# One product of two neighbouring row pairs, split once more into seven of its own quarters, in a graph network's matrix products

## The chip, the cores and the metric

The kernel runs on one core of one Trainium2 chip. The metric is the device time of one execution in microseconds (us), lower being better. TensorE multiplies matrices, VectorE (DVE in the profile), ScalarE (ACT) and GpSimd (POOL) do the rest; SyncE (SP), ACT and POOL issue DMA transfers.

## The reference

One layer of a relational graph network over 1250 nodes with 1024 features, 20000 edges of 8 types, followed by a gate; all f32.

```
h   = max(layernorm(x), 0)
u   = h @ root + bias
for r in 8 types:
    u += mean over edges of type r into each node (h[src]) @ weight[r]
z   = concat(u, h) @ w_gate + b_gate
out = x + tanh(u) * z + h * (1 - z)
```

## The kernel before, in words

The kernel multiplies first and gathers afterwards: `h` is multiplied by ten matrices of 1024 x 1024 (the eight `weight[r]`, `root`, and the half of `w_gate` that meets `h`), the products of the eight types are stored as rows in HBM (`y`, three groups of types), and rows are then gathered per edge, weighted and added into `u`. An eleventh matrix (the other half of `w_gate`) multiplies `u` at the end and is not in the loop that is changed.

**Tiling.** The 1250 nodes are 10 blocks of 128 (the last of 98). A step (s, i) multiplies matrix s (0 to 9) with pair i (0 to 4) of blocks i and i + 5, so 256 rows. Every step uses Winograd's form of Strassen's scheme: the 256 x 1024 left side and the 1024 x 1024 right side are cut into quarters, and `product` (L195) makes seven products of a 128 x 512 by a 512 x 512 quarter or sum of quarters, where a plain one takes eight. `h_op[i]` holds the left sides, transposed, under the names A11, A12, A22, S1 to S4 (A12 is block i with the second half of the features); `Factors` (L121) holds the right sides in seven buffers of 1 MB (`place`: b11, b21, b22, t1 to t4), and has two buffers more, `spare`. A matrix's b11 and t3 (which first holds b12) are loaded into the spare buffers of the matrix before (`load_first`, L134), its b22 and b21 into buffers of the matrix before as those come free. `make_t1` to `make_t4` are subtractions of whole quarters on VectorE.

**A product's order.** `product` works through A11, S1, S2, S4, S3, A12, A22. Each is four f32 matmuls of 512 columns, each of which the hardware runs as two instructions. Sums that share partial results stay in a bank of PSUM and are read in between:

```
add(b, A11, True);  copy c11 <- b      (ACT)
add(c, S1, True);   copy c22 <- c      (ACT)
add(b, S2);         copy c12 <- b      (ACT)
add(c, S4);         c12 += c           (DVE)
add(b, S3);         copy d <- b (ACT);  c22 += d (DVE)
add(a, A12, True);  c11 += a           (DVE)
add(b, A22);        copy c21 <- b      (ACT)
```

`bank()` hands out six PSUM banks in turn. The results c11 to c22 lie in two row tiles of 512 KB (`rows`, four buffers, two per step), which SP's queue stores when the step is over.

**Order of the work beside it.** Engines run their queues in the order in which the program issues instructions; that order is written by hand. After each of the seven products, `product` calls `between(j)`, in which `step` (L257) issues the handling of the next matrix and then a share of other work. In the first 440 us that is the indexing of the edges (counts and ranks, on ACT, VectorE, GpSimd and some small matmuls); after it the gathering, in which `spread` (L910) deals slots of edges over the calls: GpSimd issues an indirect DMA that gathers rows into one of four `got` buffers, and VectorE multiplies them with a weight and adds (L866). The number of calls left is counted as 7 per step. `step` calls `load_first` for the next matrix in the first step of a matrix (i = 0, j = 3); `load_b22`, `make_t1`, `load_b21` with `make_t2`, and `make_t3` come in the last step (i = 4, j = 0, 1, 3 and 4), `make_t4` at j = 0 of the next matrix's first step. All loads but those of the first matrix go through ACT's queue.

Of the kernel before, what the change touches and what calls it, by code (L numbers as in the profile page):

```python
# [9 lines left out]
F32 = mybir.dt.float32  # L10
# [9 lines left out]
def tile_rgcn_highway(  # L20
# [38 lines left out]
    KC = D // P  # L59
    KQ = KC // 2  # L60
    Q = D // 2
    ND = -(-N // P)
    NP = ND // 2
    NCH = -(-E // P)
    EL = E - (NCH - 1) * P
    G = 3
    R0 = (0, 3, 6, R)
    K = ((20, 10, 8, 7, 7, 6, 5, 5, 4, 3), (20, 10, 8, 7, 7, 6, 5, 5, 4, 3),
         (16, 7, 6, 5, 4, 4, 3, 3, 2, 2))
# [10 lines left out]
    A11, A12, A22, S1, S2, S3, S4 = range(7)  # L80
# [4 lines left out]
    def nrows(d):  # L85
        return min(P, N - d * P)
# [10 lines left out]
    rows = ctx.enter_context(tc.tile_pool(name="rows", bufs=4))  # L97
# [5 lines left out]
    hr_dram = dram.tile([N, D], F32, name="hr_dram")  # L103
    z_dram = dram.tile([N, D], F32, name="z_dram")
# [4 lines left out]
    y = [dram.tile([(R0[g + 1] - R0[g]) * N, D], F32, name=f"y{g}") for g in range(G)]  # L109
# [5 lines left out]
    def bank():  # L115
        return psum.tile([P, 512], F32, name="ps", bufs=6)
# [4 lines left out]
    class Factors:  # L121
# [3 lines left out]
        def __init__(self, w, old=None):  # L125
            self.w, self.old = w, old

        def load(self, i, j, to):
            queue = nc.scalar if self.old else nc.sync
            queue.dma_start(to, self.w[i * Q:(i + 1) * Q, j * Q:(j + 1) * Q]  # L130
                            .rearrange("(k p) n -> p k n", p=P))
            return to

        def load_first(self):  # L134
            old = self.old
            if old is None:
# [12 lines left out]
            self.load(0, 0, p["b11"])  # L149
            self.load(0, 1, p["t3"])  # L150

        def load_b22(self):
            self.load(1, 1, self.place["b22"])
# [16 lines left out]
        def make_t4(self):  # L170
            p = self.place
            nc.vector.tensor_sub(p["t4"], p["b21"], p["t2"])

    def transposed(aop, part, of, n):

        for half, to in enumerate(((A11, A12), (A21, A22))[part]):
            p = bank().rearrange("p (k f) -> p k f", k=KQ)
            for i in range(KQ):
                k = KQ * half + i
                nc.tensor.transpose(p[:, i, :n], of[:n, k * P:(k + 1) * P], ident[:n, :n])  # L180
            copy = nc.vector.tensor_copy if half else nc.scalar.copy
            copy(aop[:, to, :, :n], p[:, :, :n])  # L182
            if n < P:
                nc.gpsimd.memset(aop[:, to, :, n:], 0.0)

    def left(aop, part=0):

        if part != 3:
            nc.vector.tensor_add(aop[:, S1], aop[:, A21], aop[:, A22])
            nc.vector.tensor_sub(aop[:, S2], aop[:, S1], aop[:, A11])  # L190
        if part != 1:
            nc.vector.tensor_sub(aop[:, S4], aop[:, A12], aop[:, S2])
            nc.vector.tensor_sub(aop[:, S3], aop[:, A11], aop[:, A21])

    def product(aop, w, to, between=lambda j: None, last=None, pieces=1):  # L195

        c11, c12 = to[0][:, :Q], to[0][:, Q:]
        c21, c22 = to[1][:, :Q], to[1][:, Q:]  # L200
        step = [0]

        def add(b, i, fresh=False, at=slice(0, Q)):
            for k in range(KQ):
                nc.tensor.matmul(b[:, at], aop[:, i, k, :], w.of[i][:, k, at],  # L205
                                 start=(fresh and k == 0), stop=(k == KQ - 1),
                                 skip_group_check=True)

        def done():
            between(step[0])  # L210
            step[0] += 1

        b, c = bank(), bank()
        add(b, A11, True)
        nc.scalar.copy(c11, b)  # L215
        done()
        add(c, S1, True)
        nc.scalar.copy(c22, c)  # L218
        done()
        add(b, S2)  # L220
        nc.scalar.copy(c12, b)  # L221
        done()
        add(c, S4)
        nc.vector.tensor_add(c12, c12, c)  # L224
        done()
        add(b, S3)
        d = rows.tile([P, Q], F32, name="part", bufs=2)
        nc.scalar.copy(d, b)  # L228
        nc.vector.tensor_add(c22, c22, d)  # L229
        done()  # L230
        a = bank()
        add(a, A12, True)
        nc.vector.tensor_add(c11, c11, a)  # L233
        done()
        if pieces == 1:
            add(b, A22)
            if last:
                last(b, 0)
            else:
                nc.scalar.copy(c21, b)  # L240
        else:
            last(d, 0)
            for j in range(pieces):
                at = slice(j * Q // pieces, (j + 1) * Q // pieces)
                b = bank()
                add(b, A22, True, at)
                last(b[:, at], at.start, d[:, at])
        done()

    mats = [weight[r] for r in range(R)] + [root, w_gate[D:, :], w_gate[:D, :]]  # L250
    ROOT = R
    NM = len(mats)
    fac = []
    for w in mats:
        fac.append(Factors(w, fac[-1] if fac else None))

    def step(s, i, between=lambda j: None):  # L257

        def beside(j):
            new = fac[s + 1]  # L260
            if i == 0 and j == 0 and s > 0:
                fac[s].make_t4()
            if i == 0 and j == 3:
                new.load_first()
            if i == NP - 1:
                if j == 0:
                    new.load_b22()
                elif j == 1:
                    new.make_t1()
                elif j == 3:  # L270
                    new.load_b21()
                    new.make_t2()
                elif j == 4:
                    new.make_t3()
            between(j)

        t = [rows.tile([P, D], F32, name="row") for _ in range(2)]
        product(h_op[i], fac[s], t, between=beside)
        for part in range(2):
            d = i + part * NP  # L280
            n = nrows(d)
            at = slice(d * P, d * P + n)
            if s >= ROOT:
                to = (hr_dram, z_dram)[s - ROOT][at, :]
                nc.vector.tensor_add(t[part], t[part], bias_bc)
            else:
                g = max(k for k in range(G) if R0[k] <= s)
                o = (s - R0[g]) * N + d * P
                to = y[g][o:o + n, :]
            nc.sync.dma_start(to, t[part][:n])  # L290

    steps = iter([(s, i) for s in range(NM - 1) for i in range(NP)])

# [17 lines left out]
    h_op = [keep.tile([P, 7, KQ, P], F32, name=f"h_op{i}") for i in range(NP)]  # L311
# [58 lines left out]
    with ExitStack() as early:  # L370
# [20 lines left out]
        class Normed:  # L391
# [80 lines left out]
        for name, of, pad in (("dst", dst, G * KEYS), ("typ", etype, R), ("src", src, 0)):  # L472
            t = ix0.tile([P, 2, P], I32, name=f"e_{name}")
# [359 lines left out]
    with ExitStack() as edges_part:  # L833
        gpool = edges_part.enter_context(tc.tile_pool(name="gpool", bufs=GOT))
        upool = edges_part.enter_context(tc.tile_pool(name="upool", bufs=4))
        bias_bc = edges_part.enter_context(tc.tile_pool(name="bpool", bufs=1)).tile(
            [P, D], F32, name="bias_bc")
# [113 lines left out]
        def beside(e, total, s, i, last):  # L951


            between = spread(e, total, 7 * ((last - s) * NP + NP - i))
            while s <= last:
                step(s, i, between)
                s, i = next(steps, (NM, 0))
            return s, i
# [109 lines left out]
        def in_turn(*es):  # L1068
            for e in es:
                yield from e  # L1070
# [62 lines left out]
        def held():  # L1133

            new, old = [], []
            for _ in edges(LG, range(HELD), lambda d, u: new.append(add_hr(d, u))):
                yield
                for add in old:
                    add()
                old, new[:] = new[:], []  # L1140
            for add in old + new:
                add()

        late = edges(LG, range(HELD, ND), to_last)
        between = spread(in_turn(late, held()), sum(K[LG]) + 2, 7 * ((NM - 2 - s) * NP + NP - i))
        while s < NM - 1:
            def beside_h(j):
                between(j)
# [69 lines left out]
```

## Time and profile before

| | |
|---|---|
| median of 3 runs | 1381.52 us (1381.38 to 1381.53) |
| profiled execution, own time | 1381.64 us |
| its span, first to last instruction | 1379.8 us |
| TensorE matmuls busy (PE) | 1363.0 us, 99% |
| TensorE weight loads (PEld) | 616.9 us, 45% |
| VectorE (DVE) | 861.7 us, 62% |
| ScalarE (ACT) | 339.6 us, 25% |
| GpSimd (POOL) | 627.2 us, 45% |
| DMA | 272.73 MB, mean 198 GB/s |
| granted TensorE clock | 0.999 |

How to read the profile's rows: a group's row gives the line of the code, the engine, the operation, what is written <- what is read, the shape, the count; then the busy time in us and the mean ns of one; then the engine's idle time just before these instructions and who ended it. In a timeline row the first two numbers are the start and the duration in us, and the bracket holds the idle time before it with its releaser. Matmul records overlap[...].

### The profile page before, as it was taken

The numbers are of one execution on the slowest core, as the hardware profiler recorded it, in microseconds if no ns is written. First come the engines' busy times: TensorE is split into PE (matmuls) and PEld (weight loads), VectorE is DVE, ScalarE is ACT, GpSimd is POOL, SyncE is SP. The second block draws the span as 40 slices with busy tenths as digits, with TensorE's granted clock in tenths as the row PEclk, the third lists the DMA queues.
The fourth block names the chain that finished last, engine by engine and source line by source line (L and its number), as shares of the span: only waits on it lengthen the run. The fifth ranks groups of instructions, "written<-read, shape, count | busy, mean of one in ns | idle before, by whom it ended". The sixth has DMA issues, their size and how long they took to land.

```text
span 1379.8 us, 11992 instructions
## 1 busy us (share of the span) xinstructions
PE 1363.0 (99%) x3570; PEld 616.9 (45%) x3570; DVE 861.7 (62%) x1662; ACT 339.6 (25%) x721; POOL 627.2 (45%) x567
## 2 busy tenths in 40 slices
PE   7999999999999999999999999999999999999997
PEld 3444444444444444444444444444444444444443
DVE  6956867886768625455355485544447564557985
ACT  3335655565521111111111111111111111121220
POOL 0003655665552624556575364544426433425641
PEclk9999999999999999999999999999999999999999
DMA  8754765684645256368868656777759845656861
GB/s 302 285 203 98 172 147 114 155 181 120 101 112 173 67 166 203 77 212 198 247 225 319 203 206 246 262 286 278 251 165 333 299 158 176 206 176 234 293 201 57
DMA packets 110007, 272.73 MB, mean 198 GB/s; under 512 B 25906, under 2 KB 27936, under 8 KB 109808
## 3 DMA queue, kind: packets, MB, share of 16 engines
q0 software_dynamic: 48864, 128.60, 29.0%
q1 hardware_dynamic: 39952, 101.38, 24.9%
q10 hardware_dynamic: 21120, 41.95, 9.7%
q8 instruction: 28, 0.46, 0.2%
q14 instruction: 43, 0.35, 0.1%
HBM read 214.20 MB, written 80.65 MB: 214 GB/s over the span
## 4 chain that ended last, share of the span: by engine, by line
PE 79%; issue 7%; DVE 4%; DMA 2%; POOL 2%; ACT 1%; POOLq 0%; DVEq 0%; ACTq 0%
PE ps L205 78%; POOL got L315 1%; DMA got<-y,idx 1%; DMA w<-in_L_gnn_weight_dram 1%; DMA got<-hr_dram,node 1%; PE ps_n L605 1%; DVE row L1166 0%; DVE h_op L1103 0%; POOL out_dram L321 0%; DVE u L1066 0%; DVE row L1167 0%; PE ps_q L656 0%; DVE h_op L182 0%; DVE u L866 0%; DVE w L1103 0%
## 5 line engine op out<-in xcount | busy, mean ns | idle before, releaser
L205 PE MATMUL ps<-w,h_op 128*128 128x512 f32 (+1 forms) x3088 | 1342.4, 593 | 0.0
L205 PEld LDWEIGHTS ps<-w,h_op 128*128 128x128 f32 x3088 | 580.2, 190 | 692.7 <-issue 688.7
L866 DVE SCALAR_TENSOR_TENSOR u<-got,w_of,u 128x1024 f32<-128x1024 f32 (+1 forms) x192 | 245.9, 1282 | 213.2 <-DMA got<-y,idx 209.3
L858 POOL DMA_INDIRECT got<-y,idx x202 | 248.2, 1228 | 236.1 <-DVE u L866 149.9
L684 POOL DMA_INDIRECT table<-row_col,at_i x157 | 175.9, 1121 | 149.0 <-DVE at_i L680 69.7
L224 DVE TENSOR_TENSOR row<-row,ps 128x512 f32<-128x512 f32 x55 | 37.5, 683 | 105.8 <-PE ps L205 61.0
L228 ACT COPY part<-ps 128x512 f32<-128x512 f32 x55 | 32.2, 585 | 269.7 <-PE ps L205 266.7
L240 ACT COPY row<-ps 128x512 f32<-128x512 f32 x50 | 29.3, 585 | 251.9 <-PE ps L205 233.7
L215 ACT COPY row<-ps 128x512 f32<-128x512 f32 x55 | 32.1, 584 | 168.3 <-PE ps L205 146.0
L221 ACT COPY row<-ps 128x512 f32<-128x512 f32 x55 | 32.1, 584 | 137.8 <-PE ps L205 132.2
L218 ACT COPY row<-ps 128x512 f32<-128x512 f32 x55 | 32.1, 584 | 131.8 <-PE ps L205 125.9
L229 DVE TENSOR_TENSOR row<-row,part 128x512 f32<-128x512 f32 x55 | 37.9, 688 | 41.9 <-ACT part L228 39.7
L670 DVE SCALAR_TENSOR_TENSOR junk<-k_bc,key_col,before 128x128 f32<-128x128 int32 x157 | 54.9, 350 | 4.2
L321 POOL DMA_INDIRECT u_dram<-u,node x20 | 30.0, 1499 | 59.9 <-DVE u L866 55.3
L352 POOL DMA_INDIRECT node_dram<-ids,pos_i x30 | 37.3, 1244 | 38.6 <-issue 38.3
L610 DVE TENSOR_TENSOR seen<-seen,ps_n 128x110 f32<-128x110 f32 x157 | 42.1, 268 | 15.5 <-PE ps_n L605 10.9
L587 ACT ACTIVATE is_lo<-io,less_lo 128x128 bf16<-128x128 f32 x157 | 50.1, 391 | 0.8 <-DVE row L229 0.8
L738 DVE SCALAR_TENSOR_TENSOR junk<-v_bc,val,one 128x1280 bf16<-128x1280 f32 x30 | 46.5, 1551 | 3.9 <-DMA v_bc<-val_dram 3.2
L233 DVE TENSOR_TENSOR row<-row,ps 128x512 f32<-128x512 f32 x55 | 37.5, 682 | 18.3 <-PE ps L205 16.5
L315 POOL DMA_INDIRECT u<-u_dram,node x20 | 22.3, 1113 | 56.7 <-DMA u_dram<-u,node 41.9
L160 DVE TENSOR_TENSOR w<-w,w 128x2048 f32<-128x2048 f32 x11 | 25.2, 2290 | 28.3 <-PE ps L205 27.7
L315 POOL DMA_INDIRECT idx<-table,node_key x30 | 33.7, 1125 | 9.4 <-issue 8.5
(162 smaller groups left out, 720.3 us busy)
## 6 DMA issues: line engine op xcount, KB each, us to landing
y<-row SPq DMA_DIRECT2D x72, 512.0 KB
w<-in_L_gnn_weight_dram ACTq DMA_DIRECT2D x28, 1024.0 KB
k_bc<-keys_dram SPq DMA_DIRECT2D x39, 256.0 KB
l_bc<-los_dram SPq DMA_DIRECT2D x39, 256.0 KB
w<-in_L_gnn_w_gate_dram ACTq DMA_DIRECT2D x8, 1024.0 KB
h_dram<-h_op SPq DMA_DIRECT2D x9, 512.0 KB
hr_dram<-row SPq DMA_DIRECT2D x9, 512.0 KB
z_dram<-row SPq DMA_DIRECT2D x9, 512.0 KB
```

What stands on the lines that cost most here:

```text
L205: nc.tensor.matmul(b[:, at], aop[:, i, k, :], w.of[i][:, k, at], start=(fresh and k == 0), stop=(k == KQ - 1), skip_group_check=True)
L224: nc.vector.tensor_add(c12, c12, c)
L229: nc.vector.tensor_add(c22, c22, d)
L233: nc.vector.tensor_add(c11, c11, a)
L315: nc.gpsimd.indirect_dma_start(out=to, out_offset=None, in_=of, in_offset=bass.IndirectOffsetOnAxis(ap=at, axis=0))
L587: nc.scalar.activation(is_lo[:, i, :], io, AF.Abs, bias=less_lo[:, c0 + i:c0 + i + 1])
L610: nc.vector.tensor_add(seen[j][:, i, :], was, p[:, i, :])
L670: nc.vector.scalar_tensor_tensor(junk, o["k_bc"][:, i, :], key_col[:, c:c + 1], before, op0=OP.is_equal, op1=OP.mult, accum_out=rank[:, c: ...
L684: ins = nc.gpsimd.indirect_dma_start(out=table[:, :], out_offset=bass.IndirectOffsetOnAxis(ap=at_i[:n, i:i + 1], axis=0), in_=row_col[:n, ...
L738: nc.vector.scalar_tensor_tensor(junk, v_bc[:, g, :], val[:, c:c + 1], one.to_broadcast([P, KEYS]), op0=OP.is_gt, op1=OP.mult, accum_out=p ...
L858: nc.gpsimd.indirect_dma_start(out=t[:n], out_offset=None, in_=y[g][:, :], in_offset=bass.IndirectOffsetOnAxis(ap=at[:n, d, k:k + 1], axis=0),
L866: nc.vector.scalar_tensor_tensor(u[:n], t[:n], w, u[:n], op0=OP.mult, op1=OP.add)
```

## The change

For matrices 1 to 9, the steps i = 0 and 1, and i = 2 and 3, are taken as pairs. The A12 product of the even and of the odd step, both with b21 on the right, are taken out of `product` (`whole=False`) and made together: a 256 x 512 left side (the even step's A12 rows above the odd step's) times the 512 x 512 b21. That product is cut into quarters in its turn and made by the same scheme with seven products, each of two f32 matmuls of 256 columns (class `Second`). Step i = 4, matrix 0 and the eleventh matrix stay as they are.

- `right` makes the four differences of b21's quarters on VectorE, in the first step of a matrix, after calls 1 to 4; they go into the first spare buffer. `left` makes the four sums of the left side's quarters on VectorE after the last call (j = 5) of each even step; they go into the second spare buffer.
- `products` is a generator that the odd step advances five times: after the products A11, S1 and S2, and before the calls that follow S4 and S3. Four of the five stretches hold small matmuls, in three PSUM banks of their own; the last holds only a VectorE addition. ACT copies four partial results of 128 x 256 into the second spare buffer; VectorE adds them and the rest into c11 of both steps.
- An even step now makes 6 calls of `between`, an odd one 8, and the counts given to `spread` follow (`calls`).
- The even step's first row tile gets its A12 part only in the odd step, so it is stored there, at call 6 (`put(i - 1, 0, ...)`); the others are stored at the end of their steps.
- Since the spare buffers are used by `Second`, `load_first` of the next matrix moves, for matrices after the first, from i = 0, j = 3 to i = 3, j = 6. Its second load goes through SP's queue. `make_t1` moves from j = 1 to j = 2 of the last step.

```diff
@@ class Factors
-        def load(self, i, j, to):
-            queue = nc.scalar if self.old else nc.sync
+        def load(self, i, j, to, queue=None):
+            queue = queue or (nc.scalar if self.old else nc.sync)
...
             self.load(0, 0, p["b11"])
-            self.load(0, 1, p["t3"])
+            self.load(0, 1, p["t3"], nc.sync)
@@
+    class Second:
+        def __init__(self, f, i):
...
+            self.a11, self.a12, self.a21, self.a22 = [
+                h_op[i + o][:, A12, k:k + 2] for o in (0, 1) for k in (0, 2)]
+
+        def right(self, j):
+            to, a, b = ((self.t1, self.b12, self.b11), (self.t2, self.b22, self.t1),
+                        (self.t3, self.b22, self.b12), (self.t4, self.b21, self.t2))[j]
+            nc.vector.tensor_sub(to, a, b)
+
+        def left(self):
+            nc.vector.tensor_add(self.s1, self.a21, self.a22)
+            nc.vector.tensor_sub(self.s2, self.s1, self.a11)
+            nc.vector.tensor_sub(self.s3, self.a11, self.a21)
+            nc.vector.tensor_sub(self.s4, self.a12, self.s2)
+
+        def products(self, to):
...
+            b, c, a = [bank()[:, :H] for _ in range(3)]
+            lo, hi = slice(0, H), slice(H, Q)
+            add(b, self.a11, self.b11, True)
+            nc.scalar.copy(self.p1_p6[:, lo], b)
+            add(c, self.s1, self.t1, True)
+            nc.scalar.copy(self.p5, c)
+            yield
+            add(b, self.s2, self.t2)
+            nc.scalar.copy(self.p1_p6[:, hi], b)
+            add(c, self.s4, self.b22)
+            yield
+            add(b, self.s3, self.t3)
+            nc.scalar.copy(self.p7, b)
+            add(a, self.a12, self.b21, True)
+            more(to[0][:, :Q], self.p1_p6)
+            more(to[0][:, hi], c)
+            yield
+            add(b, self.a22, self.t4)
+            more(to[0][:, lo], a)
+            more(to[1][:, hi], self.p5)
+            more(to[1][:, hi], self.p7)
+            yield
+            more(to[1][:, lo], b)
+            yield
@@ product
+        def beside(call=False):
+            if second is not None:
+                next(second)
+                if call:
+                    done()
+
         b, c = bank(), bank()
         add(b, A11, True)
         nc.scalar.copy(c11, b)
         done()
+        beside()
         add(c, S1, True)
         nc.scalar.copy(c22, c)
         done()
+        beside(True)
         add(b, S2)
         nc.scalar.copy(c12, b)
         done()
+        beside(True)
         add(c, S4)
         nc.vector.tensor_add(c12, c12, c)
+        beside()
         done()
         add(b, S3)
         d = rows.tile([P, Q], F32, name="part", bufs=2)
         nc.scalar.copy(d, b)
         nc.vector.tensor_add(c22, c22, d)
+        beside()
         done()
-        a = bank()
-        add(a, A12, True)
-        nc.vector.tensor_add(c11, c11, a)
-        done()
+        if whole:
+            a = bank()
+            add(a, A12, True)
+            nc.vector.tensor_add(c11, c11, a)
+            done()
         if pieces == 1:
             add(b, A22)
@@ step, in beside(j)
-            if i == 0 and j == 3:
+            if two and i == 0 and 1 <= j <= 4:
+                waiting["second"].right(j - 1)
+            if two and not odd and j == 5:
+                waiting["second"].left()
+            if odd and j == 6:
+                put(i - 1, 0, waiting["to"])
+            if (s, i, j) == (0, 0, 3) or (s > 0 and i == NP - 2 and j == 6):
                 new.load_first()
             if i == NP - 1:
                 if j == 0:
                     new.load_b22()
-                elif j == 1:
+                elif j == 2:
                     new.make_t1()
```

More of the change, by code (lines that the diff above doesn't have):

```diff
@@ L61, in tile_rgcn_highway @@
     Q = D // 2
+    H = Q // 2
     ND = -(-N // P)
@@ L172, in make_t4, with add, more @@
             nc.vector.tensor_sub(p["t4"], p["b21"], p["t2"])
+    class Second:
+        def __init__(self, f, i):
+            b, f0, f1 = [t.rearrange("p k n -> p (k n)")
+                         for t in (f.place["b21"], f.spare[0], f.spare[1])]
+            b = f.place["b21"]
+            self.b11, self.b12, self.b21, self.b22 = [
+                b[:, k:k + 2, c:c + H] for k in (0, 2) for c in (0, H)]
+            self.t1, self.t2, self.t3, self.t4 = [
+                f0[:, k * Q:(k + 1) * Q].rearrange("p (k n) -> p k n", k=2) for k in range(4)]
+            self.s1, self.s2, self.s3, self.s4 = [
+                f1[:, k * H:(k + 1) * H].rearrange("p (k n) -> p k n", k=2) for k in range(4)]
+            self.p1_p6, self.p5, self.p7 = f1[:, 2 * Q:3 * Q], f1[:, 3 * Q:3 * Q + H], \
+                f1[:, 3 * Q + H:]
+            self.a11, self.a12, self.a21, self.a22 = [
[10 more added lines that the diff above has]
+        def products(self, to):
+            def add(p, a, b, fresh=False):
+                for k in range(2):
+                    nc.tensor.matmul(p, a[:, k, :], b[:, k, :], start=(fresh and k == 0),
+                                     stop=(k == 1), skip_group_check=True)
+            def more(of, a):
+                nc.vector.tensor_add(of, of, a)
+            b, c, a = [bank()[:, :H] for _ in range(3)]
[22 more added lines that the diff above has]
+            yield
@@ L193, in left, with product @@
             nc.vector.tensor_sub(aop[:, S3], aop[:, A11], aop[:, A21])
-    def product(aop, w, to, between=lambda j: None, last=None, pieces=1):
+    def product(aop, w, to, between=lambda j: None, last=None, pieces=1, whole=True,
+                second=None):
         c11, c12 = to[0][:, :Q], to[0][:, Q:]
@@ L255, in tile_rgcn_highway, with paired, calls, put @@
         fac.append(Factors(w, fac[-1] if fac else None))
-    def step(s, i, between=lambda j: None):
+    def paired(s, i):
+        return s > 0 and i < NP // 2 * 2
+    def calls(s, i):
+        return 7 if not paired(s, i) else 8 if i % 2 else 6
+    waiting = {}
+    def step(s, i, between=lambda j: None):
+        t = [rows.tile([P, D], F32, name="row") for _ in range(2)]
+        two = paired(s, i)
+        odd = two and i % 2 == 1
+        if two and not odd:
+            waiting["second"] = Second(fac[s], i)
+            waiting["to"] = t[0]
+        def put(i, part, t):
+            d = i + part * NP
+            n = nrows(d)
+            at = slice(d * P, d * P + n)
+            if s >= ROOT:
+                to = (hr_dram, z_dram)[s - ROOT][at, :]
+                nc.vector.tensor_add(t, t, bias_bc)
+            else:
+                g = max(k for k in range(G) if R0[k] <= s)
+                o = (s - R0[g]) * N + d * P
+                to = y[g][o:o + n, :]
+            nc.sync.dma_start(to, t[:n])
         def beside(j):
@@ L275, in beside @@
             between(j)
-        t = [rows.tile([P, D], F32, name="row") for _ in range(2)]
-        product(h_op[i], fac[s], t, between=beside)
+        second = waiting["second"].products((waiting["to"], t[0])) if odd else None
+        product(h_op[i], fac[s], t, between=beside, whole=not two, second=second)
         for part in range(2):
[L280 to L290, printed above, removed]
+            if part or not two or odd:
+                put(i, part, t[part])
     steps = iter([(s, i) for s in range(NM - 1) for i in range(NP)])
@@ L951, in beside @@
         def beside(e, total, s, i, last):
-            between = spread(e, total, 7 * ((last - s) * NP + NP - i))
+            between = spread(e, total, sum(calls(a, b) for a in range(s, last + 1)
+                                           for b in range(i if a == s else 0, NP)))
             while s <= last:
@@ L1144, in tile_rgcn_highway @@
         late = edges(LG, range(HELD, ND), to_last)
-        between = spread(in_turn(late, held()), sum(K[LG]) + 2, 7 * ((NM - 2 - s) * NP + NP - i))
+        between = spread(in_turn(late, held()), sum(K[LG]) + 2,
+                         sum(calls(a, b) for a in range(s, NM - 1)
+                             for b in range(i if a == s else 0, NP)))
         while s < NM - 1:
```

## The prediction

> **What bounds the kernel now.** I read the busy shares and the costliest groups of the page, then the matmuls kept apart by shape, then short stretches of the timeline.
>
> ```profile
> PE 1363.0 (99%) x3570; PEld 616.9 (45%) x3570; DVE 861.7 (62%) x1662; ACT 339.6 (25%) x721; POOL 627.2 (45%) x567
> ...
> L205 PE MATMUL ps<-w,h_op 128*128 128x512 f32 (+1 forms) x3088 | 1342.4, 593 | 0.0
> ...
> L866 DVE SCALAR_TENSOR_TENSOR u<-got,w_of,u 128x1024 f32<-128x1024 f32 (+1 forms) x192 | 245.9, 1282 | 213.2 <-DMA got<-y,idx 209.3
> ...
> L228 ACT COPY part<-ps 128x512 f32<-128x512 f32 x55 | 32.2, 585 | 269.7 <-PE ps L205 266.7
> ```
>
> The 0.0 of the matmul row says that TensorE waits for nobody; 1342.4 of the 1379.8 us span are products of L205. What shortens that stream shortens the kernel, and what puts a hole into it lengthens it. VectorE, in order, spends 209.3 us waiting for gathered rows. Two timeline rows give the price of a matmul instruction (an f32 matmul is two): a stretch of 62 of the wide form, and the weight loads of the 256-column form at the kernel's end, which keep step with their matmuls.
>
> ```profile
> 699.82 26.77 PE L205 MATMUL ps<-w,h_op 128*128 128x512 f32 x62
> ...
> 1369.10 3.21 PEld L205 LDWEIGHTS ps<-w,h_op 128*128 128x128 f32 x15 [0.24 <-issue]
> ```
>
> One matmul record lasts 592 ns, so the pitch is (26.77 - 0.592) / 61 = 0.429 us; the narrow pitch is 3.21 / 15 = 0.214 us, exactly half: 256 columns pay nothing extra for their weights. A product of eight wide instructions takes 3.43 us.
>
> [...] the trace's 256-column add at L1170 has a mean of 424. [...]
>
> **The change, part by part.**
>
> *Products.* For 18 pairs (nine matrices, two pairs each) two A12 products go: 16 x 0.429 = 6.86 us. In come seven products of 2 f32 matmuls of 256 columns: 28 x 0.214 = 6.01 us. Gain 0.86 us a pair, **15.4 us** in all, all of it on the path.
>
> *The order of what is left.* This is the step I hold decisive. Before, the A12 product stood between S3 and A22. Both of these use the same bank b, and ACT's copy at L228 reads it between them. With `whole=False` the A12 product is gone, and what the odd step runs there is only a VectorE add (the last piece of `products`). So A22's first matmul comes straight after the copy. The present crossing:
>
> ```profile
> 707.97 0.19 PEld L205 LDWEIGHTS ps<-w,h_op 128*128 128x128 f32 x1 [0.24 <-issue]
> 708.17 0.59 ACT L228 COPY part<-ps 128x512 f32<-128x512 f32 x1 [6.28 <-PE ps L205]
> ```
>
> S3's last matmul began at 707.54; the next came at pitch, at 707.97. The copy began at 708.17 and ended at 708.76. With the wait, TensorE resumes then plus a hand-over. For that the trace has one start after ACT:
>
> ```profile
> 10.16 1.52 ACT L420 ACTIVATE h_op<-xt,less,rs 128x512 f32<-128x512 f32 x2 [0.43 <-DVE less L413]
> ...
> 11.03 0.47 PE L180 MATMUL ps<-ident,h_op 128*128 128x128 f32 x1 [2.00 <-ACT h_op L420]
> ```
>
> The first of those two activations ended at 10.98 and the matmul began at 11.03, with a record 0.05 longer than its followers'; the start before it (activation ended at 6.95, matmul at 7.09) took 0.14. The hole is 708.76 + 0.14 - 707.97 = 0.93 us, between 0.8 (no hand-over) and 1.1 us (weights loaded again). There are 36 such steps: 33.5 us, ends 29 and 40. In the indexing stage (matrices 1 to 3, 12 holes) two of three calls put four small matmuls there, some 0.3 us, so about 2.6 us are covered: **+31 us**. Products and order together: +15.5 us.
>
> *VectorE.* Per matrix `right` adds 4 subtractions of 512 columns at 0.69, 2.8 us; per pair `left` 4 of 256 at 0.42, 1.7 us; the new additions are one of 512 and five of 256, 2.8 us, for two of 683 ns that go. That is 9 x 2.8 + 18 x 3.1 = 81 us more on an engine with 862 of 1380. Four 256-wide ACT copies a pair, by the nearest row at most 0.59 each, are 42 us at most on an engine at 25%. Volume fits; lateness is the matter. The second small product P5 needs `left`'s s1, queued on VectorE at the end of the even step, and comes 3.43 + 0.86 = 4.29 us after that step's last matmul. No product before depended so tightly on VectorE. How late it runs:
>
> ```profile
> 780.27 0.59 ACT L228 COPY part<-ps 128x512 f32<-128x512 f32 x1 [6.28 <-PE ps L205]
> 787.14 0.59 ACT L240 COPY row<-ps 128x512 f32<-128x512 f32 x1 [6.28 <-PE ps L205]
> ...
> 790.92 1.28 DVE L866 SCALAR_TENSOR_TENSOR u<-got,w_of,u 128x1024 f32<-128x1024 f32 x1 [16.40 <-DMA got<-y,idx]
> ...
> 802.67 0.68 DVE L233 TENSOR_TENSOR row<-row,ps 128x512 f32<-128x512 f32 x1
> ```
>
> This is the first step of matrix 6. Its last product ended at 787.1, so P5 would want s1 at 791.4; VectorE finished A12's addition, which precedes it in the queue, at 803.35. With a gather addition (1.28) and `right` and s1 (3.2) it would be ready near 808: 16 us of hole. The same reading in the first step of matrix 5 (L233 at 681.9, step's end at 666.9) gives 16, of matrix 8 (L233 19 us behind the step's end) 20, of matrix 7 about 2; elsewhere VectorE is near enough. Sum 54 us. But every hole lets VectorE catch up, so later lateness shrinks, while lateness tied to TensorE's own rows (a group's first gathers) stays. I take two thirds, **+35 us**; ends 0 and 70.
>
> *Row buffers.* The even step's first row tile is stored only at call 6 of the odd step, and the next even step reuses it after one product. Stores can be slow:
>
> ```profile
> 1057.25 0.59 ACT L215 COPY row<-ps 128x512 f32<-128x512 f32 x1 [4.94 <-DMA hr_dram<-row]
> ```
>
> There a copy waited even with a whole step's slack. Now some 10 us remain to the copy, 13 to TensorE; with a late VectorE this is a few us, inside the upper end.
>
> *Loads.* The first two quarters (1 MB each) now start at the end of the fourth step instead of early in the first, one on ACT's queue, one on SP's behind the row store, which waits for VectorE. `make_t1`, one call later than before, comes 14.7 us after. A load issued at 622.35 had only just landed when VectorE took it:
>
> ```profile
> 640.31 2.29 DVE L164 TENSOR_TENSOR w<-w,w 128x2048 f32<-128x2048 f32 x1 [0.54 <-DMA w<-in_L_gnn_weight_dram]
> ```
>
> 18 us, in a stretch with the DMA engines 90% busy. So `make_t1` can stand some 4 us and hold what is queued behind it: gather additions, `make_t2` to `make_t4`, `right`, `left`. TensorE wants t1 only five products later, so this costs nothing itself but feeds the lateness above; its relief is the lighter traffic in the first step. I count no more for it, up to 15 us at the worst. Splitting the calls 6 and 8 leaves their sum at 14: nothing.
>
> **Sum.** Profiled execution 1381.64 us (span 1379.8 and 1.84 around it) - 15.4 + 31 + 35 = 1432; the median, 1381.52, is 0.1 lower, so 1432.
>
> **Rivals.**
> A, forecast, 0.62: bank hole and late VectorE both count, 1412 to 1455.
> B, 0.22: VectorE's lateness goes under (the changed load times remove it, or TensorE's 0.9 us holes let it keep up); only the bank hole: 1381.6 + 15.5 = 1397, with a few us of lateness up to 1412. Against it speak the 16 us wait shown above.
> C, 0.12: loads squeezed into one step throttle the gathers, `make_t1` blocks, and each matrix of the edge stage loses 10 us and more: 1455 to 1485. For it speaks the 18 us load.
> D, faster, 0.04: the wait on bank b costs less than 15.4 / 36 = 0.43 us a step, the point from which the sign turns, with VectorE in time: at best 1381.6 - 15.4 = 1366. That needs the resume to come before the 0.59 us copy is over; the copy's row speaks against it.
>
> **Numbers.** What a measurement of this kernel can tell from no change is about 0.2%, 2.8 us. The range from 1397 to 1465 leaves out the lower part of B with D, and the upper part of C. Faster 0.03, same 0.01, slower 0.96.
>
> **What would show it.** In the changed profile: the matmul row's idle no longer 0.0 but 50 to 90 us, released by ACT at the L228 copy in 36 holes near 0.93 us; a second set of holes before P5 released by VectorE's `left`, in the first pairs of matrices 5, 6 and 8; the narrow matmuls at 0.214 us. If those holes are missing, or the narrow form's pitch is well above 0.214 us, the reasoning is wrong.

## The result: 59 us slower, and the profile after

The changed kernel takes 1440.68 us (median of 4 runs, 1439.36 to 1444.99) against 1381.45 us of the kernel before: a ratio of 1.0435, 95% interval 1.0413 to 1.0457. Its profiled execution has a span of 1438.4 us, 58.6 more than before.

Line numbers shift from kernel to kernel: L274 is now the matmul of `product` (L205 before, L276 in most of the experiments), L307 ACT's copy after S3, L974 the gather addition; L210 is the matmul of the small products, L201 the first line of `left`. The page of the changed kernel has these rows in the place of those shown of before:

```profile
PE 1364.3 (95%) x3786; PEld 658.0 (46%) x3786; DVE 927.2 (64%) x1842; ACT 365.6 (25%) x793; POOL 621.0 (43%) x567
...
L274 PE MATMUL ps<-w,h_op 128*128 128x512 f32 x2800 | 1238.0, 596 | 25.5 <-ACT part L307 22.9
...
L974 DVE SCALAR_TENSOR_TENSOR u<-got,w_of,u 128x1024 f32<-128x1024 f32 (+1 forms) x192 | 245.8, 1282 | 185.0 <-DMA got<-y,idx 183.3
...
L307 ACT COPY part<-ps 128x512 f32<-128x512 f32 x55 | 32.2, 585 | 294.0 <-PE ps L274 294.0
L210 PE MATMUL ps<-w,w 128*128 128x256 f32 x288 | 74.0, 390 | 29.2 <-DVE w L201 29.2
```

The matmul row's idle time was 0.0; now it is 25.5 us, nearly all released by ACT's copy, and the small products have 29.2 us of their own, released by `left`. TensorE's list of waits counts them (what waits, for whom, us in total, how often, the longest):

```profile
PE ps L210 <- DVE w L201: 29.2, 4, 15.5
PE ps L274 <- ACT part L307: 22.9, 35, 1.0
...
PE ps_n L713 <- DVE seen L718: 2.8, 1, 2.8
PE ps L274 <- DVE w L174: 1.3, 1, 1.3
PE ps L274 <- DVE w L162: 1.0, 1, 1.0
```

A stretch of TensorE's timeline shows both in the first two steps of matrix 5, and a row of ACT and three of VectorE beside it show who was late (P1 is the first small product, P5 the second, which needs the sum s1 that `left` makes):

```profile
659.74 8.75 PE L274 MATMUL ps<-w,h_op 128*128 128x512 f32 x20
669.16 7.13 PE L274 MATMUL ps<-w,h_op 128*128 128x512 f32 x16 [0.68 <-ACT part L307]
676.13 1.03 PE L210 MATMUL ps<-w,h_op 128*128 128x256 f32 x4
687.43 2.07 PE L210 MATMUL ps<-w,w 128*128 128x256 f32 x4 [10.28 <-DVE w L201]
689.30 5.22 PE L274 MATMUL ps<-w,h_op 128*128 128x512 f32 x8
694.36 1.89 PE L210 MATMUL ps<-w,w 128*128 128x256 f32 x8
696.09 3.60 PE L274 MATMUL ps<-w,h_op 128*128 128x512 f32 x8
```

```profile
668.52 0.59 ACT L307 COPY part<-ps 128x512 f32<-128x512 f32 x1 [6.28 <-PE ps L274]
...
675.74 1.29 DVE L974 SCALAR_TENSOR_TENSOR u<-got,w_of,u 128x1024 f32<-128x1024 f32 x1 [9.47 <-DMA got<-y,idx]
...
683.22 1.28 DVE L974 SCALAR_TENSOR_TENSOR u<-got,w_of,u 128x1024 f32<-128x1024 f32 x1 [3.20 <-DMA got<-y,idx]
...
686.96 0.42 DVE L201 TENSOR_TENSOR w<-h_op 128x256 f32<-128x256 f32 x1
```

ACT's copy ends at 669.11, and at 669.16 A22 resumes, 0.68 us after S3's last record ended; a record outlasts the pitch by 0.16 (0.592 against 0.429), so the hole is 0.84 us. At 677.16 P1 is done and P5 wants s1; VectorE had stood 9.47 us before a gathered row and 3.20 before another, and made s1 at 686.96. The eight narrow matmuls from 694.36 give way to a wide one at 696.09, so their pitch is 0.216 us. Another row shows something else: 8 wide matmuls from 689.30 last 5.22 us, where 8 at the pitch of 0.429 would last 3.6, as those from 696.09 do. The table by stretches has the granted clock (the number before the DMA share):

```profile
687.00:691.00 4.00, 3.57 (x6) 2.18 (x7) 3.34 (x7) 0.37 (x1) 2.05 (x3) 0.50 0.91 348
...
1081.00:1085.00 4.00, 4.00 (x7) 2.43 (x8) 4.00 (x6) 0.37 (x1) 1.55 (x1) 0.50 0.33 101
```

After these two long holes, of 10.28 us and of 15.52 us (in matrix 8), TensorE ran at half its clock (0.50 in both rows). Put together, in us, with 0.16 added to every idle time to make it a hole:

| part of the 58.6 us | us |
|---|---|
| matmuls at their pitches, 0.429 and 0.216 (2784 wide and 504 narrow for 3072 wide, two records for each f32 matmul) | -14.7 |
| 35 holes for ACT's copy | +28.6 |
| 4 holes before P5 (10.4, 2.2, 1.5, 15.7) | +29.8 |
| a count in the indexing stage, and three waits for t1, t2, t4 | +6 |
| matmuls at a halved clock (excess over the pitch, 7.1 against 1.5 before) | +6 |
| what remains, not traced further | +3 |

### The profile page after: what moved, and what is told of

It is laid out like the page before. It is cut to its first block, busy times and chain, and to the rows that moved or that the text cites. A ratio compares the mean times of both kernels' runs of the same rounds, so it can differ in the third digit from the quotient of the medians.

```text
span 1438.4 us, 12754 instructions
## 1 busy us (share of the span) xinstructions
PE 1364.3 (95%) x3786; PEld 658.0 (46%) x3786; DVE 927.2 (64%) x1842; ACT 365.6 (25%) x793; POOL 621.0 (43%) x567
## 3 DMA queue, kind: packets, MB, share of 16 engines
q0 software_dynamic: 48864, 128.60, 28.6%
## 4 chain that ended last, share of the span: by engine, by line
PE 42%; issue 24%; DMA 11%; POOL 9%; DVE 8%; ACT 2%; POOLq 0%; DVEq 0%; ACTq 0%
PE ps L274 37%; DMA got<-y,idx 6%; PE ps L210 5%; POOL got L966 4%; DMA u<-u_dram,node 2%; DVE u L974 2%; POOL u_dram L429 1%; POOL got L423 1%; DMA w<-in_L_gnn_weight_dram 1%; ACT part L307 1%; DMA got<-hr_dram,node 1%; POOL u L423 1%; DMA node_dram<-ids,pos_i 1%; PE ps_n L713 0%; POOL node_dram L460 0%
## 5 line engine op out<-in xcount | busy, mean ns | idle before, releaser
L274 PE MATMUL ps<-w,h_op 128*128 128x512 f32 x2800 | 1238.0, 596 | 25.5 <-ACT part L307 22.9
L274 PEld LDWEIGHTS ps<-w,h_op 128*128 128x128 f32 x2800 | 525.4, 191 | 643.5 <-issue 586.0
L974 DVE SCALAR_TENSOR_TENSOR u<-got,w_of,u 128x1024 f32<-128x1024 f32 (+1 forms) x192 | 245.8, 1282 | 185.0 <-DMA got<-y,idx 183.3
L966 POOL DMA_INDIRECT got<-y,idx x202 | 243.5, 1205 | 270.5 <-DVE u L974 176.4
L302 DVE TENSOR_TENSOR row<-row,ps 128x512 f32<-128x512 f32 x55 | 37.7, 685 | 121.4 <-PE ps L274 72.0
L307 ACT COPY part<-ps 128x512 f32<-128x512 f32 x55 | 32.2, 585 | 294.0 <-PE ps L274 294.0
L210 PE MATMUL ps<-w,w 128*128 128x256 f32 x288 | 74.0, 390 | 29.2 <-DVE w L201 29.2
L210 PEld LDWEIGHTS ps<-w,w 128*128 128x128 f32 x288 | 54.8, 194 | 49.8 <-DVE w L201 30.8
L321 ACT COPY row<-ps 128x512 f32<-128x512 f32 x50 | 29.2, 585 | 183.4 <-PE ps L274 177.5
L294 ACT COPY row<-ps 128x512 f32<-128x512 f32 x55 | 32.2, 585 | 143.5 <-PE ps L274 139.5
L460 POOL DMA_INDIRECT node_dram<-ids,pos_i x30 | 40.3, 1344 | 40.0 <-issue 39.4
L210 PE MATMUL ps<-w,h_op 128*128 128x256 f32 x216 | 55.7, 380 | 0.0
L210 PEld LDWEIGHTS ps<-w,h_op 128*128 128x128 f32 x216 | 40.7, 190 | 19.0 <-issue 14.6
```

Of the source, the lines that this page charges most:

```text
L210: nc.tensor.matmul(p, a[:, k, :], b[:, k, :], start=(fresh and k == 0), stop=(k == 1), skip_group_check=True)
L460: ins = nc.gpsimd.indirect_dma_start(out=node_dram[g][:, :], out_offset=bass.IndirectOffsetOnAxis(ap=pos_i[:, g, d:d + 1], axis=0), in_=id ...
L966: nc.gpsimd.indirect_dma_start(out=t[:n], out_offset=None, in_=y[g][:, :], in_offset=bass.IndirectOffsetOnAxis(ap=at[:n, d, k:k + 1], axis=0),
L974: nc.vector.scalar_tensor_tensor(u[:n], t[:n], w, u[:n], op0=OP.mult, op1=OP.add)
```

## Experiments

All ratios are against runs of the kernel before that were made beside the experiment's, with 95% intervals.

**e1_hole_alone.** Is the order alone worth 30 us? The kernel before, without any of the split:

```diff
+        if early:                 # s > 0 and i < 4
+            by_a12()
         add(b, S3)
         nc.scalar.copy(d, b)
         ...
-        by_a12()
+        if not early:
+            by_a12()
         add(b, A22)
```

> The kernel before, with nothing of the change but one reordering: in the 36 steps that the change pairs, the A12 product is made before S3 instead of after it, so that A22 follows S3 directly, on the bank that ACT still copies. Same matmuls, same additions, same stores. Theory (the wait for the copy opens a hole of 0.84 us over the pitch, as in 27 places of the changed kernel's trace): 36 holes, some of those in the indexing stage partly filled by small matmuls, so 1381.5 + 28 = 1409 us (1405 to 1413), and no other new wait. Rival (the holes of the changed kernel come from its late VectorE or its fuller ACT queue, not from the order): within 3 us of 1381.5.

Measured: 1413.36 us, 1.0229 (1.0212 to 1.0246), so +31.9 us, 0.89 us for each of 36 holes and just above the theory's range. In its list of TensorE's waits nothing else is new, and the clock stays at 0.999:

```profile
PE ps L205 <- ACT part L236: 23.0, 36, 0.7
```

With 0.16 added to each, the waits are 28.8 of the 31.9 us; the rest is not traced. This settles the bank hole: no small product and no late VectorE is needed for it. Holes of 0.84 us did not bring the clock down: it is 1.00 in each of three stretches from 40 to 1320 us.

**e2_hole_covered.** The same hole from the other side: small products are laid into it. The short diff is of the changed kernel; the lines that hand the small products over from the even to the odd step are left out.

```diff
             add(b, self.a11, self.b11, True)      # even step, after S3
             nc.scalar.copy(self.p1_p6[:, lo], b)
+            yield
             add(c, self.s1, self.t1, True)        # odd step, after A11
...
-            add(b, self.a22, self.t4)
             more(to[0][:, lo], a)
             more(to[1][:, hi], self.p5)
             more(to[1][:, hi], self.p7)
             yield
+            add(b, self.a22, self.t4)             # odd step, after S3
             more(to[1][:, lo], b)
```

> The changed kernel, with the small products P1 moved between S3 and A22 of the even step, and the last small product moved between S3 and A22 of the odd step: 0.86 us of matmuls lie where the bank wait was. left stays late, and P5 now starts 3.43 instead of 4.29 us after the even step. Theory (two separate causes that add up): the bank holes, some 29 us, go; the four waits for left grow by 0.9 us each, to some 33 us; 1440.7 - 29 + 3 = 1415 us (1409 to 1421). Rival (the holes only gave VectorE time to catch up, and what is taken there comes back before P5): waits for left rise to 45 us and over, 1427 to 1440.

Measured: 1427.18 us, 1.0329 (1.0312 to 1.0346), 13.5 us better than the changed kernel where the theory said 26. That is the lower end of the rival's range:

```profile
PE ps L210 <- DVE w L201: 43.1, 5, 17.3
...
PE ps L276 <- ACT part L309: 0.3, 2, 0.2
```

The copy's waits fell from 22.9 to 0.3, but the waits for `left` rose from 29.2 to 43.1. An estimated 4 us of that rise come from P5 itself, which now starts 0.86 us earlier in each of the places; the rest fits the rival, that the small holes had given VectorE time to catch up.

**e3_left_early.** The other cause by itself:

```diff
-            if two and not odd and j == 5:
+            if two and not odd and j == 0:
                 waiting["second"].left()
```

> The changed kernel, with left issued on VectorE after the first call of the even step (j = 0) instead of after its last (j = 5), five products earlier in VectorE's queue; nothing else. Theory: the 29.8 us of waits before P5 go, and with them the slow matmuls after the long ones (some 5 us): 1440.7 - 35 = 1406 us (1402 to 1412); the 36 bank holes stay. Rival (the next thing on the late VectorE, the difference t1 or the row store that waits for it, stops TensorE in its place): 1420 to 1438.

Measured: 1420.26 us, 1.0271 (1.0254 to 1.0289): 20 us better, not 35, on the edge of the rival. The waits for `left` are gone; in their place stand waits that the changed kernel had shorter or not at all, t4 above all, and a copy (L294) that had no row buffer yet:

```profile
PE ps L274 <- DVE w L174: 4.7, 1, 4.7
PE ps_n L713 <- DVE seen L718: 3.0, 1, 3.0
PE ps L274 <- ACT row L294: 2.6, 1, 2.6
```

**e4_both.** Both edits together.

> The changed kernel with both moves: small products between S3 and A22, and left after the first call of the even step. Theory: what is left is the gain of the split, 15.4 us, less a few us of other new waits (small matmuls of the counts, make_t's, 0.1 us hiccups, together some 8 us in the changed kernel's trace): 1366 to 1378 us, so faster than before. Rival (a third cost was hidden behind the two, such as the loads squeezed into one step or the late row store): over 1381.5.

Measured: 1405.16 us, 1.0194 (1.0159 to 1.0229). The rival again: still 24 us slower than before, with a list of short waits, each for another thing:

```profile
PE ps L210 <- DVE w L198: 5.8, 3, 2.9
PE ps L276 <- ACT row L296: 4.4, 1, 4.4
PE ps L276 <- DVE w L174: 3.5, 1, 3.5
PE ps_n L720 <- DVE seen L725: 3.3, 1, 3.3
PE ps L276 <- DVE row L214: 2.6, 1, 2.6
```

(L198 is `right`, L296 the copy into c22, L174 `make_t4`, L720 the counting of edges, L214 an addition that frees a bank.) These are 20 us; the matmuls at a halved clock now carry 11.2 us of excess, against 1.5 before. So a third cost was there. Two candidates: the loads squeezed together, or VectorE's lateness in a matrix's first steps.

**e5_late_loads.** The kernel before, with only the loads moved:

```diff
-            if i == 0 and j == 3:
+            if (s, i, j) == (0, 0, 3) or (s > 0 and i == NP - 2 and j == 6):
                 new.load_first()
...
-                elif j == 1:
+                elif j == 2:
                     new.make_t1()
```

and the second load on SP's queue, as in the change.

> The kernel before with the changed kernel's load times alone: for matrices after the first, the next matrix's first two quarters load at the end of the fourth step (one through SP's queue) and make_t1 comes one call later; no small products, the old order. Theory (the loads in one step make VectorE later, but nothing of the old order depends on that tightly): 1381.5 to 1384.5 us, TensorE's waits for VectorE under 3 us in all. Rival (the squeezed loads are the third cost that e4_both showed; make_t1 and what follows come too late for TensorE): 1387 to 1402.

Measured: 1389.09 us, 1.0049 (1.0032 to 1.0065), +7.3: the rival's range. Most of it is lost in one place, in the indexing stage, at the end of matrix 1. VectorE first, then TensorE:

```profile
269.10 2.29 DVE L164 TENSOR_TENSOR w<-w,w 128x2048 f32<-128x2048 f32 x1 [5.02 <-DMA w<-in_L_gnn_weight_dram]
...
277.58 1.18 DVE L610 TENSOR_TENSOR seen<-seen,ps_n 128x110 f32<-128x110 f32 x4
```

```profile
278.81 0.53 PE L605 MATMUL ps_n<-is_at,is_lo 128*128 128x110 bf16 x4 [3.25 <-DVE seen L610]
279.12 6.54 PE L205 MATMUL ps<-w,h_op 128*128 128x512 f32 x8
```

`make_t2` stands 5.02 us before its quarter of the matrix; the counts queue behind it on VectorE (L661 runs at 271.31, on the result of a matmul of 262.67); the next counting matmul finds its one PSUM bank still unread and waits 3.25 us; and then eight matmuls take 6.54 us instead of 3.6 (the mean clock of this run is 0.997, that of the runs of before beside it 0.998 to 0.999). The same wait is in the changed kernel (L713, 2.8 us; the clock stayed at 1.00 there) and in e2_hole_covered to e4_both (3.0, 3.0 and 3.3 us). A wait of 1.0 us for t1, at the first step of matrix 8, is the largest of the others that are new. Which of the three moves (the later loads, the other queue, the later `make_t1`) does it was not tried apart.

**e6_second_pair** and **e7_first_pair.** e4_both with half of the pairs, to part the two candidates:

```diff
-        return s > 0 and i < NP // 2 * 2
+        return s > 0 and i in (2, 3)      # e6_second_pair; e7_first_pair: (0, 1)
```

In e7_first_pair `load_first` moves to i = 1, j = 6.

> e4_both with the small products in the second pair of each matrix only (i = 2 and 3); the first pair is made as before, right still runs in the first step, the loads stay late. Half of the gain, 7.7 us. Theory (what is left in e4_both is VectorE's lateness in a matrix's first steps, where gathers and make_t's pile up[...]): the first pair's waits go, two or three waits of 3 us stay: 1374 to 1384 us. Rival (late loads): they are all still there, so 1388 to 1400.

> e4_both with the small products in the first pair of each matrix only (i = 0 and 1); the second pair is made as before, and the next matrix's first loads start at the end of the second step, so that they are spread as widely as the split allows. Half of the gain, 7.7 us. Theory (lateness in the first steps): the waits stay, some 15 us with the slow clock: 1386 to 1398 us. Rival (late loads): the early loads remove them: 1373 to 1381.

Measured: 1394.01 us, 1.0071 (1.0048 to 1.0094) and 1396.04 us, 1.0109 (1.0087 to 1.0131); the first varies from 1385 to 1400, and its profile is of a run of 1400. For the second pair the rival's range was right: with the first pair gone, the counts' wait of 3.3 us is still there, and two waits for a row buffer, 13.3 us together, are the largest. The first of them, in ACT's and SP's timelines of e6_second_pair:

```profile
743.00 0.37 ACTq L132 DMA_DIRECT2D w<-in_L_gnn_weight_dram  x1
754.70 0.59 ACT L296 COPY row<-ps 128x512 f32<-128x512 f32 x1 [11.14 <-DMA y<-row]
```

```profile
745.44 0.32 SPq L376 DMA_DIRECT2D y<-row  x1
746.31 0.47 SPq L132 DMA_DIRECT2D w<-in_L_gnn_weight_dram  x1
```

The held row goes out at 745.44, between two loads of 1 MB issued at 743.00 (b22, which the change does not move) and 746.31, and its buffer is wanted again one step later; ACT gets it at 754.70, and TensorE stands 5.6 us behind ACT. How much of this the loads cause is not shown: the store itself came late, since VectorE ended its addition into that row only at 745.41, and in e8_more_slack TensorE waits 3.9 us for a row buffer in the third step of matrix 5, where no weight load is near. For the first pair the theory was right: with earlier loads a wait of 7.1 us for t1 (L198) is left, at the first steps of matrix 8. So each pair keeps waits of its own; the second pair's were not parted between the loads and VectorE.

**e8_more_slack.** Can the slack be had by order alone? e4_both with t1, and `left` with it, made ahead of t4, and P5 one product later (not in the short diff):

```diff
+            if two and not odd and j == 0:
+                if i == 0:
+                    waiting["second"].right(0)
+                waiting["second"].left()
             if i == 0 and j == 0 and s > 0:
                 fac[s].make_t4()
-            if two and i == 0 and 1 <= j <= 4:
-                waiting["second"].right(j - 1)
-            if two and not odd and j == 0:
-                waiting["second"].left()
+            if two and i == 0 and 1 <= j <= 3:
+                waiting["second"].right(j)
```

> e4_both with t1 made first of all on VectorE in a matrix's first step (ahead of make_t4) and the small product P5 made after S1 of the odd step instead of after A11; S4 times b22 and the last two follow one product later each. From t1's place in VectorE's queue to P5 there are then some 25 us of matmuls, before 18. Theory: the waits for t1 (6.3 us in e4_both's trace, and the slow clock after them, about 5) go, the rest stays: 1390 to 1397 us. Rival (VectorE's lateness just stops TensorE at the next thing: t4, a row buffer, a PSUM bank): over 1400.

Measured: 1407.58 us, 1.0189 (1.0172 to 1.0206): nothing won, and the rival's range. No wait for t1 is left; t4, which it was put ahead of, is waited for 7.4 us instead of 3.5. In VectorE's queue, where the counts of e5_late_loads stood behind a wait of 5.02 us, what was pulled forward pushed something else back.

**e9_chosen_pairs** and **e10_index_and_store.** If the places are known, leave them out. Both are e4_both with the loads of matrix 1 early again, as in the kernel before, and with

```diff
-        return s > 0 and i < NP // 2 * 2
+        return s > 1 and i < 4 and (i > 1 or s not in (5, 6, 8))    # e9
+        return s > 1 and i < NP // 2 * 2                            # e10
...
+            else:
+                put(i, part, t[part], slice(Q, D))    # the done half of the held row
```

> e4_both with the small products only where the traces showed no wait before them: matrix 1 made as before and with early loads; in matrices 5, 6 and 8 only the second pair, with right in the second step; both pairs in 2, 3, 4, 7 and 9: 13 pairs, so a gain of 13 x 0.86 = 11.2 us. The even step's held row tile is stored in two halves, the half that is done at the end of the even step. Theory (each remaining loss in e4_both has its place: the counts behind late loads in matrix 1, VectorE late at the first steps of 5, 6 and 8, the slow store of a held row): the waits named go, some 5 us of hiccups and one or two waits stay: 1372 to 1380 us. Rival (lateness moves to whatever depends on it next): 1382 to 1395.

> e4_both with two of these steps alone: matrix 1 made as before with early loads, and the held row tile stored in two halves; 16 pairs, 13.7 us of gain, all pairs of matrices 2 to 9. Theory: the wait of the counts at 278 us and its slow clock (6 us) and the wait for the row store (4.5 us and some 3 of slow clock) go, 1.7 us of gain are given up; the waits at the first steps of matrices 5, 6 and 8 stay: 1405 - 12 = 1393 us (1389 to 1398). Rival: the store isn't what was waited for, or the wait moves on: 1399 to 1405.

Measured: e10_index_and_store 1394.95 us, 1.0097 (1.0082 to 1.0112), within the theory's range but not by all of its reasons: the counts' wait is gone, the wait for the row buffer (L296) is still 5.7 us, so halving the store did not remove it. e9_chosen_pairs 1385.94 us, 1.0037 (1.0024 to 1.0050), the rival's range. Its runs lie between 1379.93 and 1388.22 us; in its profiled one, of 1379.93 us, a single wait of size is left, for a held row in matrix 7; what the others lost is not known:

```profile
PE ps L276 <- ACT row L296: 5.1, 1, 5.1
```

**e11_calm_matrices.** The pairs of matrices 2, 3, 4 and 9 alone; 1 and 5 to 8 as before, early loads included:

```diff
-        return s > 1 and i < 4 and (i > 1 or s not in (5, 6, 8))
+        return s in (2, 3, 4, 9) and i < NP // 2 * 2
```

> e9_chosen_pairs narrowed further: small products (both pairs, covered holes, left early, held row stored in halves) in matrices 2, 3, 4 and 9 alone, where no run showed a wait before them; matrices 1 and 5 to 8 wholly as before, with early loads. 8 pairs, a gain of 8 x 0.86 = 6.9 us. Theory (the losses of e9_chosen_pairs come from the gathering stage of matrices 5 to 8, by amounts that vary from run to run): they go, 2 to 3 us of hiccups stay: 1374 to 1379 us, faster than before by 0.2 to 0.5%. Rival (each pair costs about what it gains, wherever it stands): 1380 to 1385.

Measured: 1375.14 us, 0.9960 (0.9947 to 0.9974): faster than the kernel before by 6.1 us, where 8 pairs are worth 6.5 at the pitch of 0.216. Matrix 3 was not as free of waits as the expectation says (e2_hole_covered 2.1 us, e7_first_pair 3.4 us), but here the matmuls, kept apart by shape, wait for nobody:

```profile
L276 PE MATMUL ps<-w,h_op 128*128 128x512 f32 x2944 | 1288.3, 595 | 0.0
L210 PE MATMUL ps<-w,w 128*128 128x256 f32 x128 | 32.0, 382 | 0.0
L210 PE MATMUL ps<-w,h_op 128*128 128x256 f32 x96 | 24.6, 379 | 0.0
```

So the split itself gives nearly what it counts for, 0.76 us a pair of 0.82, once its holes are covered and `left` comes early; what the table has against it in the changed kernel lies in what the split is hung on.

## Why the prediction was right, step by step

- **Total.** 1432 us forecast, 1440.7 measured, by the mechanism named as the likeliest. That the sum came so near is in part luck: order and VectorE together came out 7.6 us smaller than forecast, and some 15 us that no term had (the last three rows of the table) more than made up for it.
- **Products**, -15.4 us: -14.7. The narrow pitch was read too short: 3.21 us are 14 pitches and the last load's 0.19 us, so 0.216 and not 3.21 / 15 = 0.214. e11_calm_matrices got 6.1 us for 8 pairs, of 6.5. Right but for that.
- **Order**, +31 us, 0.93 us a hole: +28.6 us in the trace, 0.84 us a full hole, and +31.9 us in e1_hole_alone, which has nothing else in it. Right; the trace of before had shown no matmul waiting for a copy out of its bank, so that it would was the author's estimate; the row of waits shows it 36 times in e1_hole_alone, 23.0 us in all. The 0.09 us too much is the hand-over: of the two that the trace had shown, 0.05 and 0.14 us, the changed kernel has the shorter one.
- **VectorE**, +35 us from 54: 29.8 us, in matrices 5 to 8 as named. The single sizes were worse than the sum: 16, 16, 2 and 20 forecast for those four, 10.4, 2.2, 1.5 and 15.7 measured. Nothing had measured the two thirds by which the sum was cut, so that it fits is in part chance. That holes let VectorE catch up agrees with e2_hole_covered: with the bank holes filled the waits for s1 rose to 43.1 us.
- **Loads**, nothing by themselves: this step failed. "TensorE wants t1 only five products later, so this costs nothing itself" looked at the gathering stage only. In the indexing stage the counts stand behind `make_t2` on VectorE and TensorE waits for them: the larger part of the +7.3 us in e5_late_loads, some 3 us in the changed kernel. In the gathering stage too the changed kernel waits for t1, t2 and t4 in matrix 8, 2.7 us in all.
- **Row buffers**, a few us: none in the changed kernel; 2.6 to 13.3 us in the profiles of e3_left_early, e4_both and e6_second_pair to e10_index_and_store, once the earlier holes were gone.
- **Missing: the clock.** No step priced that a long hole costs more than its length, as the two of 10.28 and 15.52 us did with the clock of 0.50 after them. The 6 us of the table were not in the sum.

## What to carry to other kernels

Before taking a product out of a stream that bounds a kernel, look at what stood behind it: here a matmul group that is read halfway and continued waited for that read wherever no other group's matmuls lay between, and the product that went was that cover, worth 0.89 us a time in e1_hole_alone. New operands made by an engine that often waits, as VectorE does here (185.0 us before gather additions in the changed kernel), should be issued as early as their inputs allow, and their slack compared with the worst lateness in the trace, stage by stage; a change that pays in calm stages can be kept to them.

## What the runs showed of the hardware that was not expected

In these traces half the clock followed idle time of TensorE, but the length of a hole alone did not decide. In e4_both a wait of 1.94 us was followed by half the clock (0.50), in e7_first_pair one of 3.37 us was not (1.00) (rows of the timelines, and of the tables by stretches):

```profile
1049.41 2.03 PE L210 MATMUL ps<-w,w 128*128 128x256 f32 x4 [1.94 <-DVE w L198]
...
1049.50:1052.90 3.40, 3.40 (x6) 2.06 (x7) 1.89 (x2) 0.37 (x1) 2.31 (x3) 0.50 0.90 302
```

```profile
463.72 6.71 PE L276 MATMUL ps<-w,h_op 128*128 128x512 f32 x15 [3.37 <-ACT row L296]
...
463.72:467.50 3.78, 3.78 (x9) 1.82 (x10) 3.67 (x7) 0.44 (x1) 0.00 (x0) 1.00 1.13 222
```

In the changed kernel too a wait of 2.07 us (before 814.59) was followed by half the clock, one of 2.79 us (before 277.07) by the full one. What parts them is in the records of the granted clock. The stretches at half clock between the first and the last products of the changed kernel last 10.24, 3.41 and 17.07 us, each a multiple of 3.413 us, and begin at 682.32, 815.44 and 1068.02, 39 and 74 times 3.413 us apart, so on one grid. In that trace a cell of this grid at full clock in which TensorE had no matmul running for up to 1.86 us was followed by the full clock, and one with 2.07 us or more by half. The 1.94 us of e4_both lie in one cell, which half the clock followed; the 3.37 us of e7_first_pair fall on two, 1.42 and 1.95, which it did not follow, and the 2.79 us of the changed kernel as 1.86 and 0.94. The 36 waits of e1_hole_alone, of up to 0.7 us, never brought the clock down (1.00 from 40 to 1320 us). So a cell did not have to be idle throughout: 2.07 us of its 3.413 were enough in the changed kernel and 1.94 in e4_both, while 1.95 were not in e7_first_pair.
